# The first group's front of an RWKV-6 block: load order, norm, centering and mixing placed differently

## The chip, the cores and the metric

The kernel runs on one core of one Trainium2 chip. The metric is the device time of one execution in microseconds. Before the change it is 1533.85 us, the median of three runs (1533.52 to 1534.64).

A core has five engines with a queue each, worked in order: TensorE (PE in the profile; its weight loads are shown as PEld), VectorE (DVE), ScalarE (ACT), GpSimd (POOL) and SyncE (SP), which only issues DMAs here. ACT issues some DMAs too. "PEq", "SPq" and the like are the sequencers of the engines.

## The reference

The input is x with 32 sequences of 128 tokens and 512 features, and a context that supplies, for each sequence, two previous rows and a 16 x 512 starting state. All is float32. Cut to what matters:

```python
xn = ln(x) * ln1_w + ln1_b
sx = token_shift(xn, prev)                      # previous row minus this row
xxx = tanh((xn + sx * maa_x) @ maa_w1)          # 5 parts of 32
xxx = matmul(xxx, maa_w2)                       # 5 parts of 512
x5  = xn + sx * (maa_stack + xxx)               # five mixed inputs
w = exp(-exp(time_decay + tanh(x5[1] @ decay_w1) @ decay_w2))
r, k, v = x5[3] @ Wr.T, x5[0] @ Wk.T, x5[2] @ Wv.T
g = silu(x5[4] @ Wg.T)
# per head (32 heads of 16): s is 16 x 16
a = k_t * v_t (outer);  out_t = r_t . (u * a + s);  s = a + w_t * s
att = groupnorm_per_head(out) * gn_w + gn_b
x = x + (att * g) @ Wo.T
xn2 = ln(x) * ln2_w + ln2_b;  sx2 = token_shift(xn2, prev2)
x = x + sigmoid((xn2 + sx2*fmr) @ Wfr.T) * (square(relu((xn2 + sx2*fmk) @ Wfk.T)) @ Wfv.T)
```

## The kernel before, in words

The 32 sequences are worked in eight groups of four. A group's rows are one tile `x` of 128 tokens by 4 x 512 (`load_x`, L283). After the norm everything of the front is held transposed: 128 features on the partitions, four chunks of features (index e or f), and 4 x 128 tokens along the free axis.

For each group there are five generators: `front_mix` (L422) norms, shifts and mixes; `front_proj` (L492) computes the decay w and the projections k, r, v; `front_gate` computes the gate; `prep` (L567) prepares the recurrence; `back` does the group norm, the output projection, the second norm and the feed-forward part. Six more generators do the recurrence over all groups, one unit after another: POOL multiplies k and v (L704) and adds pairs (L708), DVE scans (L726) and multiplies by r (L728), PE sums (L761). Before each instruction a generator yields an `Op`: an engine, a duration in us, the buffers it reads and writes, and sometimes a condition (`need`). `Plan.run` (L138) plays these Ops in a model of the engines when the kernel is built. At each step it takes, among the generators whose next Op could start within EPSILON of the earliest, the one with the smallest due time (`pick`, L177). The due times come from the table DUE (L49): for each kind of generator a begin and an end, in units of groups. So DUE, EPSILON and the durations in the Ops decide the order of the instructions in every queue of the whole kernel; on the chip each engine works that order and waits where data are not there.

The parts that the change touches:

- `load_x` issues one DMA of 1 MB on SP for a group's rows. Two `x` tiles exist.
- `constants` (L247) runs once, in the first group's `front_mix`. It issues the loads of `vec` (all per-feature vectors, L248), `pv` (previous rows, L253), `w1` (L255), the halves of `maa_w2` on SP and on ACT (L259), the decay weights (L262, L264) and `u` (L267), and has POOL compute the four small `ffn` vectors from `vec` (L249 to L252).
- `weight` (L289) issues the load of 1 MB of weights on SP. For the first group `front_proj` asks for wv, wk and wr at once (L497 to L501).
- `center` (L296) subtracts, on POOL, each head's mean from the columns of wv (L303 to L310) and writes the result to DRAM (`dwv`, L312), from where later groups load it.
- `layernorm_T` (L319): for each sequence statistics on DVE (L332, L333); `rstd` on DVE (L350), its power -1/2 on POOL (L352), `nb` on DVE (L354); then the norm, four ACT instructions (L357); a copy of `pv` on ACT (L361); PE transposes chunk by chunk (L377). For each chunk ACT evicts with ln weight and bias into `xnT` (`evict`, L367), then `use` of `front_mix` has ACT do the same in place (L433), DVE subtract to `sx` (L436) and DVE make `xin` (L438, tile `mx`).
- In `front_mix`, PE then multiplies `xin` by `w1` (L444, L397), ACT takes the tanh (L448 to L456), and for each of five inputs m and each pair of chunks PE multiplies by `maa_w2` (L410) and `mixed` (L460) works the two chunks. There are two ways to do one: in groups 1 to 7, for m in `ON_POOL`, DVE does L465 and POOL the addition L467; otherwise DVE does both, L470 and L472. In the first group all five m take the second way.

```python
                if g and m in ON_POOL:
                    nc.vector.scalar_tensor_tensor(x5[:, f, :], p.t, col(V_MAA + m, f), sx[:, f, :], ALU.add, ALU.mult)
                    nc.gpsimd.tensor_tensor(bt(x5[:, f, :]), bt(x5[:, f, :]), row(xnT, f, 1), ALU.add)
                else:
                    nc.vector.scalar_tensor_tensor(p.t, p.t, col(V_MAA + m, f), sx[:, f, :], ALU.add, ALU.mult)
                    nc.vector.tensor_tensor(bt(x5[:, f, :]), bt(p.t), row(xnT, f, 1), ALU.add)
```

Of the kernel before, what the change touches and what calls it, by code (L numbers as in the profile page):

```python
# [19 lines left out]
GB = 4  # L20
# [22 lines left out]
LANDING = 2.0  # L43
HOP = (0.2, 0.05, 0.05, 0.04, 0.08)
ON_POOL = (2, 3, 4)
EPSILON = 0.0388


DUE = {"rec": (0.171, 1.108), "mix": (-4.67, -2.417), "proj": (-4.683, 4.311), "gate": (0.588, 0.608), "prep": (-4.19, 1.684), "back": (-0.012, 3.928), "last1": (-21.388, 9.796), "last2": (10.392, 13.665)}  # L49


class Buf:
# [130 lines left out]
def rwkv6_block(ctx: ExitStack, tc: tile.TileContext, x, prev, s0, vecs, u, maa_w1, maa_w2,  # L183
# [61 lines left out]
    nc.vector.memset(w2p, 0.0)  # L245

    def constants():  # L247
        nc.sync.dma_start(out=vec, in_=vecs)  # L248
        nc.gpsimd.tensor_scalar(ffn[:, 0, :], vec[:, V_FK, :], -1.0, 1.0, ALU.mult, ALU.add)  # L249
        nc.gpsimd.tensor_scalar(ffn[:, 2, :], vec[:, V_FR, :], -1.0, 1.0, ALU.mult, ALU.add)  # L250
        nc.gpsimd.tensor_tensor(ffn[:, 1, :], ffn[:, 0, :], vec[:, V_LN2B, :], ALU.mult)
        nc.gpsimd.tensor_tensor(ffn[:, 0, :], ffn[:, 0, :], vec[:, V_LN2W, :], ALU.mult)  # L252
        nc.sync.dma_start(out=pv, in_=prev)  # L253
        halves = lambda w, h: w.rearrange("r (f h p) -> h r f p", h=2, p=P)[h]
        nc.sync.dma_start(out=w1_sb, in_=maa_w1.rearrange("(c p) o -> p c o", p=P))  # L255
        for m in (1, 0, 2, 3, 4):
            for h, queue in enumerate((nc.sync, nc.scalar)):
                r = h * XD + (XM if m in (1, 3) else 0)
                queue.dma_start(out=w2p[r : r + XM, m, :].rearrange("r (f p) -> r f p", p=P),  # L259
                                in_=halves(maa_w2[m * XM : (m + 1) * XM, :], h))  # L260
            if m == 1:
                nc.sync.dma_start(out=dw1_sb, in_=decay_w1.rearrange("(c p) o -> p c o", p=P))  # L262
                for h, queue in enumerate((nc.sync, nc.scalar)):
                    queue.dma_start(out=dw2p[h * XD : (h + 1) * XD, :].rearrange("r (f p) -> r f p", p=P),  # L264
                                    in_=halves(decay_w2, h))
        for e in range(NE):
            nc.sync.dma_start(out=lanes(u_sb, e), in_=u[e * HE : (e + 1) * HE, :].unsqueeze(0).to_broadcast([GB, HE, S]))  # L267

    def lanes(t, e):


        return t[e::NE]
# [4 lines left out]
    def bt(ap):  # L277
        return ap.rearrange("p (b t) -> p b t", t=L)
# [3 lines left out]

    def load_x(g, need=None, bs=range(GB)):  # L283
        b0, b1 = bs[0], bs[-1] + 1
        (xt,) = yield Op(SP, 0.4, w=[(0, None)], alloc=["x"], xfer=part(4.5, bs), need=need)
        nc.sync.dma_start(out=xt[:, b0:b1, :], in_=x[g * GB + b0 : g * GB + b1].rearrange("b t e -> t b e"))
        return xt
# [27 lines left out]
    def part(us, bs):  # L315

        return us if len(bs) == GB else us * len(bs) / GB + 0.03

    def layernorm_T(g, src, sums, vw, vb, which, use, take, need=None, bs=range(GB)):  # L319
# [33 lines left out]
        (nb,) = yield Op(DVE, 0.16, r=[(mv, None), (rstd, None)], w=[(0, None)], alloc=["nb"], port=True, end=[mv])  # L353
        nc.vector.scalar_tensor_tensor(nb[:, bsl], mean, -1.0 if sums is None else 1.0, rstd[:, bsl], ALU.mult, ALU.mult)  # L354
        for b in bs:
            yield Op(ACT, 0.8, r=[(src, b), (nb, None), (rstd, None)], w=[(xh, b)])
            nc.scalar.activation(xh[:, b, :], src[:, b, :], AF.Identity, bias=nb[:, b : b + 1],  # L357
                                 scale=rstd[:, b : b + 1])
# [4 lines left out]
        late = []  # L363

        def evict(e, pt):
            yield Op(ACT, part(0.78, bs), r=[(pt, None)], w=[(xnT, e)])
            nc.scalar.activation(xnT[:, e * GB + b0 : e * GB + b0 + nb_, 1 : L + 1], bt(pt[:, cols]), AF.Identity,  # L367
                                 bias=col(vb, e), scale=col(vw, e))
            yield from use(xnT, e, pt, tiles)

        for e in range(NE):
# [50 lines left out]
    def front_mix(g, d):  # L422

        xt = yield from load_x(g, (lambda: "x1" in data[g - 3]) if g > 2 else (lambda: "xin" in data[0]) if g else None)
        if g == 0:
            yield Op(SP, 5.5, xfer=4.0)
            yield Op(ACT, 3.9)
            constants()
        need = (lambda: "ln2" in data[g - 3]) if g > 2 else None
        def use(xnT, e, pt, tiles):  # L430

# [7 lines left out]

        xnT, sx, xin = yield from layernorm_T(g, xt, None, V_LN1W, V_LN1B, 0, use, ("sx", "mx"), need)  # L440
        d["xin"] = True
        (pm,) = yield Op(PE, 8 * PASS, r=[(xin, None)], w=[(0, None)], alloc=["ps"])
        for c in range(NE):
            nc.tensor.matmul(pm.t, lhsT=w1_sb[:, c, 0 : 4 * XM], rhs=xin[:, c, :], start=(c == 0), stop=(c == NE - 1))  # L444
# [15 lines left out]
        def mixed(m, i, pp, x5):  # L460

            for f, p in zip((2 * i, 2 * i + 1), pp):
                if g and m in ON_POOL:
                    yield Op(DVE, 0.75, r=[(p, None), (sx, None)], w=[(x5, f)], end=[p])
                    nc.vector.scalar_tensor_tensor(x5[:, f, :], p.t, col(V_MAA + m, f), sx[:, f, :], ALU.add, ALU.mult)  # L465
                    yield Op(POOL, 1.08, r=[(xnT, None)], w=[(x5, f)], port=True)
# [25 lines left out]
    def front_proj(g, d):  # L492
# [507 lines left out]
```

## Time and profile before

| | |
|---|---|
| runs | 1533.85 us (1533.52 to 1534.64) |
| profiled execution | 1535.0 us, of which the span of the instructions is 1533.2 |
| mean granted TensorE clock | 0.959 |
| busy: PE, DVE, POOL, ACT | 1410.0, 1270.9, 1024.8, 656.2 us |
| rows of group 0: issue, first use | 0.72, 6.12 us |
| last `xin` of group 0 done | 26.23 us |
| first mixing instruction on DVE | 37.51 us |
| first projection (k) | 62.52 us |
| first recurrence instruction (POOL L704) | 109.16 us |
| last group's recurrence done, about | 1451 us |

The profile is one execution. Its instructions have a start (us from the start of the span), a duration, the engine, the line of the kernel and the tiles, written before "<-" and read behind it. What ended an engine's idle time is inferred from semaphores. The chain that ended last is followed back from the last instruction. Matmuls are pipelined and their ends are modelled, so busy time of PE is not time at its peak. A float32 matmul of 128x512 appears as two records.

### The profile page before, as it was taken

How to read it: one execution, taken by the hardware profiler on the slowest of the kernel's cores; microseconds unless marked ns; L12 is line 12 of the kernel's file. 1: busy time of each engine (PE TensorE's matmuls, PEld its weight loads, DVE VectorE, ACT ScalarE, POOL GpSimd, SP SyncE). 2: the span in 40 equal slices, each digit the busy share in tenths (PEclk: the TensorE clock that was granted, in tenths of full speed). 3: DMA queues.
4: the chain of work that ended last, by engine and by line, in shares of the span. 5: the costliest groups of instructions: out<-in, count | busy, mean ns of one | idle time of the engine just before them, and what ended most of it. 6: DMA issues, size and time to landing. Idle time of an engine off the chain costs nothing.

```text
span 1533.2 us, 16578 instructions
## 1 busy us (share of the span) xinstructions
PE 1410.0 (92%) x5344; PEld 746.6 (49%) x5344; DVE 1270.9 (83%) x1618; ACT 656.2 (43%) x1277; POOL 1024.8 (67%) x632
## 2 busy tenths in 40 slices
PE   3997898899999999999999999999999998778788
PEld 1343454455554555455554555455544555455444
DVE  5537789989998899899988899899988898878732
ACT  4233242423743356323743365424733354344242
POOL 3014893877787859687786959686777959678400
PEclk9798899899999999999999999999999999889879
DMA  6120331244304431244304521343305421400220
GB/s 223 42 84 23 104 108 29 78 132 145 117 11 144 144 131 43 79 133 142 117 29 134 183 92 35 97 140 124 110 32 163 126 89 41 159 27 28 93 71 28
DMA packets 127559, 146.88 MB, mean 96 GB/s; under 512 B 8176, under 2 KB 77296, under 8 KB 126448
## 3 DMA queue, kind: packets, MB, share of 16 engines
q1 hardware_dynamic: 92112, 128.81, 25.6%
q10 hardware_dynamic: 35360, 17.02, 3.9%
q8 instruction: 42, 0.69, 0.2%
q14 instruction: 45, 0.37, 0.1%
HBM read 94.41 MB, written 17.83 MB: 73 GB/s over the span
## 4 chain that ended last, share of the span: by engine, by line
PE 51%; DVE 27%; POOL 13%; issue 6%; DMA 2%; ACT 1%; SPq 1%; DVEq 0%; POOLq 0%; ACTq 0%
PE ps L391 18%; PE acc L761 8%; POOL am L704 7%; PE ps L939 6%; PE ps L923 6%; PE ps L410 6%; DVE sc L726 5%; POOL a L708 4%; DVE rm L728 4%; PE ps L849 2%; DVE rk L642 2%; DVE ps L634 2%; PE ps L397 2%; PE ps L444 2%; DVE ps L470 1%
## 5 line engine op out<-in xcount | busy, mean ns | idle before, releaser
L704 POOL TENSOR_TENSOR am<-v,k 128x1024 f32<-128x1024 f32 x256 | 610.3, 2384 | 88.7 <-DMA r<-blk 70.4
L391 PE MATMUL ps<-mx,wt 128*128 128x512 f32 (+1 forms) x1312 | 583.2, 593 | 8.8 <-DVE mx L472 3.4
L708 POOL TENSOR_TENSOR a<-am 128x504 f32<-128x504 f32 x256 | 286.1, 1118 | 201.5 <-DVE sc L726 181.1
L391 PEld LDWEIGHTS ps<-mx,wt 128*128 128x128 f32 x1312 | 244.3, 194 | 276.2 <-issue 259.1
L728 DVE TENSOR_TENSOR rm<-sc,r 128x1024 f32<-128x1024 f32 x256 | 312.9, 1222 | 38.3 <-PE acc L761 22.9
L726 DVE TENSOR_TENSOR_SCAN sc<-sc,a 128x512 f32<-128x512 f32 x256 | 313.4, 1224 | 32.7 <-POOL a L708 30.5
L761 PE MATMUL acc<-by_head,rm 128*128 128x128 f32 x2176 | 290.8, 283 | 36.0 <-DVE rm L728 29.9
L761 PEld LDWEIGHTS acc<-by_head,rm 128*128 128x128 f32 x2176 | 252.3, 146 | 135.9 <-issue 54.4
L679 ACT COPY sc<-w 128x512 f32<-128x512 f32 x256 | 151.4, 591 | 219.5 <-DVE rm L728 197.0
L690 ACT COPY a<-st 128x8 f32<-128x8 f32 x256 | 52.2, 204 | 180.1 <-DVE sc L726 156.4
L467 POOL TENSOR_TENSOR mx<-mx,xnT 128x512 f32<-128x512 f32 x84 | 99.7, 1198 | 40.9 <-DVE mx L465 40.3
L923 PE MATMUL ps<-wt,mx 128*128 128x512 f32 x256 | 115.7, 595 | 0.0
L540 ACT COPY blk<-ps 128x512 f32<-128x512 f32 x96 | 56.0, 584 | 137.6 <-PE ps L391 137.6
L849 PE MATMUL ps<-wt,mx 128*128 128x512 f32 x256 | 112.8, 598 | 0.6 <-DVE rk L642 0.6
L410 PE MATMUL ps<-tha,w2p 64*128 64x512 f32 x256 | 89.1, 677 | 18.0 <-DVE mx L472 12.0
L939 PE MATMUL ps<-wt,ev 128*128 128x512 f32 x224 | 102.4, 600 | 2.7 <-DVE mx L472 2.7
L352 POOL TENSOR_TENSOR rstd<-rstd,mhalf 128x4 f32<-128x4 f32 (+1 forms) x17 | 20.2, 1191 | 120.1 <-DVE rstd L350 120.1
L470 DVE SCALAR_TENSOR_TENSOR ps<-ps,vec,sx 128x512 f32<-128x512 f32 x76 | 57.3, 753 | 36.7 <-PE ps L410 36.3
L465 DVE SCALAR_TENSOR_TENSOR mx<-ps,vec,sx 128x512 f32<-128x512 f32 x84 | 61.8, 743 | 21.8 <-PE ps L410 21.7
L849 PEld LDWEIGHTS ps<-wt,mx 128*128 128x128 f32 x256 | 48.9, 192 | 62.5 <-issue 56.5
L923 PEld LDWEIGHTS ps<-wt,mx 128*128 128x128 f32 x256 | 46.4, 190 | 51.0 <-issue 46.8
L939 PEld LDWEIGHTS ps<-wt,ev 128*128 128x128 f32 x224 | 40.9, 192 | 45.3 <-issue 39.9
(108 smaller groups left out, 1341.1 us busy)
## 6 DMA issues: line engine op xcount, KB each, us to landing
x<-in_x SPq DMA_DIRECT2D x15, 1024.0 KB
wt<-in_wk SPq DMA_DIRECT2D x8, 1024.0 KB
wt<-in_wr SPq DMA_DIRECT2D x8, 1024.0 KB
wt<-in_wg SPq DMA_DIRECT2D x8, 1024.0 KB
dgate<-blk SPq DMA_DIRECT2D x32, 256.0 KB
wt<-in_wo SPq DMA_DIRECT2D x8, 1024.0 KB
wt<-in_fk SPq DMA_DIRECT2D x8, 1024.0 KB
wt<-in_fr SPq DMA_DIRECT2D x8, 1024.0 KB
```

What stands on the lines that cost most here:

```text
L391: nc.tensor.matmul(p, lhsT=w[:, c, e * P : (e + 1) * P], rhs=xin[:, c, cols], start=(c == 0), stop=(c == NE - 1))
L410: nc.tensor.matmul(p.t, lhsT=w[h, :], rhs=t[h, :], start=True, stop=True)
L467: nc.gpsimd.tensor_tensor(bt(x5[:, f, :]), bt(x5[:, f, :]), row(xnT, f, 1), ALU.add)
L679: nc.scalar.copy(sc.t, d["w01"][:, q : q + 1, :].to_broadcast([P, DH, T2]))
L704: nc.gpsimd.tensor_tensor(am.t, v[:, ds, :], k[:, q : q + 1, :].to_broadcast([P, DH, L]), ALU.mult)
L708: nc.gpsimd.tensor_tensor(a[:, :, 1:T2], am2[:, :, 0 : T2 - 1, 0], am2[:, :, 0 : T2 - 1, 1], ALU.add)
L726: nc.vector.tensor_tensor_scan(scf, scf, a.t.rearrange("p d n -> p (d n)"), 0.0, ALU.mult, ALU.add)
L728: nc.vector.tensor_tensor(pair(rm.t), sc.t.unsqueeze(3).to_broadcast([P, DH, T2, 2]), r2[:, q : q + 1, :, :].to_broadcast([P, DH, T2, 2]), ...
L761: nc.tensor.matmul(acc[:, i, :], lhsT=rm[:, i, :], rhs=by_head, is_transpose=True, start=(q == 0 and i % 4 == 0), stop=(q == S), skip_grou ...
L849: nc.tensor.matmul(p.t, lhsT=att[:, c, b * L : (b + 1) * L], rhs=wot[:, c, :], start=(c == 0), stop=(c == NE - 1))
L923: nc.tensor.matmul(p.t, lhsT=xr[:, c, b * L : (b + 1) * L], rhs=frt[:, c, :], start=(c == 0), stop=(c == NE - 1))
L939: nc.tensor.matmul(p2.t, lhsT=kv[:, c, b * L : (b + 1) * L], rhs=fvt[:, c, :], start=(c == 0), stop=(c == NE - 1))
```

## The change

Seven edits, all but the last for the first group only:

- Its rows are loaded in two DMAs: sequences 0 and 1 on SP, 2 and 3 on ACT. `vec` and `pv` follow on ACT's queue.
- `constants` no longer issues `vec`, `pv` and `u` and no longer computes `ffn`; wv is asked for only after the constants, and `u` after the weights of the first group (in `prep`).
- The `ffn` vectors are computed by `of_norm2`, behind the norm.
- The norm of sequences 1 and 3 is done by DVE, that of 0 and 2 by ACT.
- The eviction with ln weight and bias is done by DVE in place of ACT.
- In the mixing of every m, the odd chunks take the way with the addition on POOL.
- DUE and EPSILON have other values. (The condition of `center` on "xin" is as it was.)

```diff
-EPSILON = 0.0388
+EPSILON = 0.039
-DUE = {"rec": (0.171, 1.108), "mix": (-4.67, -2.417), "proj": (-4.683, 4.311), "gate": (0.588, 0.608), "prep": (-4.19, 1.684), "back": (-0.012, 3.928), "last1": (-21.388, 9.796), "last2": (10.392, 13.665)}
+DUE = {"rec": (0.171, 0.811), "mix": (-4.351, -2.486), "proj": (-6.56, 7.24), "gate": (0.525, 0.545), "prep": (-4.001, 1.375), "back": (-0.209, 3.178), "last1": (-27.722, 1.84), "last2": (7.448, 22.404)}
...
     def constants():
-        nc.sync.dma_start(out=vec, in_=vecs)
-        nc.gpsimd.tensor_scalar(ffn[:, 0, :], vec[:, V_FK, :], -1.0, 1.0, ALU.mult, ALU.add)
...
-        nc.sync.dma_start(out=pv, in_=prev)
...
-        for e in range(NE):
-            nc.sync.dma_start(out=lanes(u_sb, e), in_=u[e * HE : (e + 1) * HE, :].unsqueeze(0).to_broadcast([GB, HE, S]))
+    def of_norm2():
+        nc.gpsimd.tensor_scalar(ffn[:, 0, :], vec[:, V_FK, :], -1.0, 1.0, ALU.mult, ALU.add)
+        nc.gpsimd.tensor_scalar(ffn[:, 2, :], vec[:, V_FR, :], -1.0, 1.0, ALU.mult, ALU.add)
+        nc.gpsimd.tensor_tensor(ffn[:, 1, :], ffn[:, 0, :], vec[:, V_LN2B, :], ALU.mult)
+        nc.gpsimd.tensor_tensor(ffn[:, 0, :], ffn[:, 0, :], vec[:, V_LN2W, :], ALU.mult)
...
     def load_x(g, need=None, bs=range(GB)):
+        if g == 0:
+            (xt,) = yield Op(SP, 0.4, w=[(0, 0), (0, 1)], alloc=["x"], xfer=2.3)
+            nc.sync.dma_start(out=xt[:, 0:2, :], in_=x[0:2].rearrange("b t e -> t b e"))
+            yield Op(ACT, 1.4, w=[(xt, 2), (xt, 3)], xfer=2.3)
+            nc.scalar.dma_start(out=xt[:, 2:4, :], in_=x[2:4].rearrange("b t e -> t b e"))
+            nc.scalar.dma_start(out=vec, in_=vecs)
+            nc.scalar.dma_start(out=pv, in_=prev)
+            return xt
...
         for b in bs:
+            if g == 0 and sums is None and b % 2:
+                yield Op(DVE, 0.5, r=[(src, b), (nb, None), (rstd, None)], w=[(xh, b)], port=True)
+                nc.vector.tensor_scalar(xh[:, b, :], src[:, b, :], rstd[:, b : b + 1], nb[:, b : b + 1], ALU.mult, ALU.add)
+                continue
...
         def evict(e, pt):
+            if g == 0 and sums is None:
+                yield Op(DVE, 0.69, r=[(pt, None)], w=[(xnT, e)])
+                nc.vector.tensor_scalar(xnT[:, e * GB + b0 : e * GB + b0 + nb_, 1 : L + 1], bt(pt[:, cols]), col(vw, e), col(vb, e), ALU.mult, ALU.add)
+            else:
...
...
         if g == 0:
-            yield Op(SP, 5.5, xfer=4.0)
+            yield Op(SP, 5.0, xfer=4.0)
             yield Op(ACT, 3.9)
             constants()
+            d["constants"] = True
...
         d["xin"] = True
+        if g == 0:
+            yield Op(POOL, 0.9)
+            of_norm2()
...
-                if g and m in ON_POOL:
+                if m in ON_POOL if g else f % 2:
...
         if g == 0:
-            ws[2] = yield from weight(wv)
+            ws[2] = yield from weight(wv, lambda: "constants" in d)
             plan.add(center(ws[2]), -1.0, -0.9, 8)
             ws[0] = yield from weight(wk)
             ws[3] = yield from weight(wr)
+            d["weights"] = True
...
     def prep(g, d):
+        if g == 0:
+            yield Op(SP, 2.5, need=lambda: "weights" in d)
+            for e in range(NE):
+                nc.sync.dma_start(out=lanes(u_sb, e), in_=u[e * HE : (e + 1) * HE, :].unsqueeze(0).to_broadcast([GB, HE, S]))
```

More of the change, by code (lines that the diff above doesn't have):

```diff
@@ L247, in constants @@
     def constants():
-        nc.sync.dma_start(out=vec, in_=vecs)
[L249 to L252, printed above, removed]
-        nc.sync.dma_start(out=pv, in_=prev)
         halves = lambda w, h: w.rearrange("r (f h p) -> h r f p", h=2, p=P)[h]
@@ L365, in evict @@
         def evict(e, pt):
-            yield Op(ACT, part(0.78, bs), r=[(pt, None)], w=[(xnT, e)])
-            nc.scalar.activation(xnT[:, e * GB + b0 : e * GB + b0 + nb_, 1 : L + 1], bt(pt[:, cols]), AF.Identity,
-                                 bias=col(vb, e), scale=col(vw, e))
+            if g == 0 and sums is None:
+                yield Op(DVE, 0.69, r=[(pt, None)], w=[(xnT, e)])
+                nc.vector.tensor_scalar(xnT[:, e * GB + b0 : e * GB + b0 + nb_, 1 : L + 1], bt(pt[:, cols]),
+                                        col(vw, e), col(vb, e), ALU.mult, ALU.add)
+            else:
+                yield Op(ACT, part(0.78, bs), r=[(pt, None)], w=[(xnT, e)])
+                nc.scalar.activation(xnT[:, e * GB + b0 : e * GB + b0 + nb_, 1 : L + 1], bt(pt[:, cols]), AF.Identity,
+                                     bias=col(vb, e), scale=col(vw, e))
             yield from use(xnT, e, pt, tiles)
```

## The prediction

> **What bounds the kernel now.** I read the engine totals first, then the busy time by stretch, then the chain that ended last for the first 130 us, then the instructions in order of time there, and last the waits. The totals and four stretches (columns: stretch, its length, busy time and instruction count of PE, PE's weight loads, DVE, ACT, POOL, the granted TensorE clock, DMA share, GB/s):
>
> ```profile
> PE 1410.0 (92%) x5344; PEld 746.6 (49%) x5344; DVE 1270.9 (83%) x1618; ACT 656.2 (43%) x1277; POOL 1024.8 (67%) x632
> ...
> 37.50:62.50 25.00, 20.39 (x48) 6.67 (x48) 20.84 (x33) 10.16 (x17) 1.01 (x1) 0.70 0.16 43
> ...
> 109.20:300.00 190.80, 164.30 (x605) 82.07 (x603) 157.98 (x189) 66.36 (x140) 133.93 (x81) 0.90 0.21 64
> 300.00:1250.00 950.00, 931.86 (x3651) 493.09 (x3650) 870.38 (x1099) 437.70 (x851) 720.83 (x437) 0.99 0.33 107
> 1250.00:1451.00 201.00, 168.98 (x702) 102.00 (x699) 160.78 (x171) 83.75 (x163) 154.07 (x91) 0.93 0.21 70
> ```
>
> From 300 to 1250 us TensorE is busy 931.9 of 950 us (98.1%): that middle holds only 18 us in which a late start could be caught up. So a start that comes earlier moves the whole middle, and with it the end. The start itself is not bound by TensorE. Instructions in order of time (start, duration, engine, line, tiles; in brackets the engine's idle time and what ended it):
>
> ```profile
> 6.12 0.69 DVE L332 BATCH_NORM_STATS2 stats<-x 128x6 f32<-128x512 f32 x1 [3.94 <-DMA x<-in_x]
> ...
> 9.44 0.17 DVE L350 TENSOR_SCALAR rstd<-mv 128x4 f32<-128x4 f32 x1
> ...
> 11.13 0.19 POOL L249 TENSOR_SCALAR ffn<-vec 128x4 f32<-128x4 f32 x1 [8.88 <-DMA vec<-in_vecs]
> ...
> 11.87 1.02 POOL L352 TENSOR_TENSOR rstd<-rstd,mhalf 128x4 f32<-128x4 f32 x1
> ...
> 12.87 2.32 POOL L303 TENSOR_TENSOR am<-wt 128x1024 f32<-128x1024 f32 x1
> 12.93 2.27 DVE L354 SCALAR_TENSOR_TENSOR nb<-mv,rstd 128x4 f32<-128x4 f32 x1 [3.31 <-POOL rstd L352]
> ...
> 15.24 2.93 ACT L357 ACTIVATE x<-x,nb,rstd 128x512 f32<-128x512 f32 x4 [7.71 <-DVE nb L354]
> ...
> 25.48 0.75 DVE L438 SCALAR_TENSOR_TENSOR mx<-sx,vec,ps 128x512 f32<-128x512 f32 x1
> ...
> 30.18 0.69 DVE L332 BATCH_NORM_STATS2 stats<-x 128x6 f32<-128x512 f32 x1 [3.95 <-DMA x<-in_x]
> ```
>
> Three things are to be seen. The power (L352) is ready to run at 9.61 and runs at 11.87, behind four `ffn` instructions that wait for `vec`. The tiny `nb` instruction takes 2.27 us, where its later executions take 0.15 to 0.16: it ends with POOL's 2.32 us L303, which began 0.06 us before it. And at 26.23 DVE stops for 3.95 us for the rows of the second group, then takes the statistics of groups 1 and 2, before it mixes group 0. The chain shows what that costs (start, length, what):
>
> ```profile
> 21.10 9.05 DMA x<-in_x
> 30.18 0.70 DVE stats L332
> ...
> 37.60 0.67 DVE ps L470
> ...
> 62.52 15.92 PE ps L391 x32
> ```
>
> Mixing starts at 37.51, the first projection (k) at 62.52. In between TensorE has a granted clock of 0.70 and waits for DVE:
>
> ```profile
> PEld ps L410 <- DVE mx L472: 20.4, 11, 7.9
> ```
>
> POOL's recurrence starts at 109.16, when the lanes of v have landed.
>
> **Part by part.** *Rows on two queues.* The one load is issued at 0.72 and its statistics start at 6.12. The Trainium skill ("DMA: Bandwidth & Descriptors", section "Rules for kernel authors") speaks against this edit: spreading loads over issuing engines gives no bandwidth, since all run on the same 16 DMA engines; only issue time is saved. Issue is 0.44 us here. By the trace alone one could hope for half of the transfer, some 1.3 us (1 MB at about 400 GB/s is 2.6 us; 376 GB/s is what the stretch from 20 to 30 us moves). I take the rule: both halves land at about 6.1, gain 0; behind SP's half now stands 0.3 MB of `w1` in place of 1 MB of `wv`, so no loss is seen either. Range 1 us either way.
>
> *Vectors ahead of weights, `ffn` behind the norm.* The power runs at 9.65 instead of 11.87 and ends at 10.67. The centering is placed behind it in POOL's queue, and `wv` is issued behind the constants, so at 10.7 no long POOL instruction runs: `nb` takes 0.16 and ends at 10.86 instead of 15.20. Gain 4.3 (2.2 of wait for `vec`, 2.1 of collision). The 10 us of centering and the 0.8 of `ffn` (4 x 0.2) move behind; their cover is long, since the centered weights are first used at 83.9 and `ffn` after the first recurrence. If `wv` were in by 10.7, L303 would collide again: 2.3 lost. ACT issues three more DMAs (0.44 + 0.34 + 0.34 = 1.1 us). Its own old ones begin only at 2.21, so most of this lies in idle time; it is free at about 6.2 with a table load of 1.28 behind, and first needed at 10.9. If ACT were held up as SP was (4.4 us, 1.72 to 6.11), its half of the norm would be 1 us late.
>
> *`u` moved.* Its four issues (2.42 us on SP, 15.21 to 17.63) go behind wk and wr, before the states and x of groups 1 and 2. First use is L639 at 122.9, so nothing waits; the weights come 2.4 us sooner, the rows behind them do not.
>
> *Norm shared.* Four ACT instructions of 0.73 (2.93 in all) become two on ACT, 1.47, beside two on DVE. No row has this DVE form; the nearest at that size is L472 with 0.69, a floor is half of it; two take 0.7 to 1.4, hidden beside ACT. Gain 1.5.
>
> *Eviction on DVE.* Until now ACT carries two instructions per chunk (0.77 + 0.75) and DVE two (0.69 + 0.75); from the first eviction (18.73) to the last `xin` (26.23) it is 7.5 us. Now DVE carries 0.69 + 0.69 + 0.75 = 2.13, four times 8.5. ACT's part waits for DVE's read, but the next eviction can fill that gap on DVE. Loss 1.0, up to 2.5 if the gaps stay open. Last `xin` at 10.86 + 1.47 + 0.56 (transposes, as from 18.17 to 18.73) + 8.6 = 21.5, so 4.7 us sooner than 26.23.
>
> *Statistics of groups 1 and 2 ahead of the mixing.* From the last `xin` to the first mixing pair TensorE and the tanh need 4.1 us (26.23 to about 30.3), so DVE could mix at 25.6. The eight statistics take 7.3 us (30.18 to 37.43). If they stay ahead and x1 is there by 21.5, mixing starts at 29.0. x1 was issued at 21.10 because SP stood still for 7.7 us (1.72 to 6.11, 6.45 to 8.41, 8.75 to 10.13) behind x and wv before it could issue the constants. Now `vec` and `pv` are on the other queue and a smaller half of x is ahead: I put the constants' issue (5.1 us) at about 2 to 8, the three weights and x1 behind them (4 MB at 376 to 400 GB/s, 10.6 us) at about 10 to 21, with landing 20 to 23. Ends for the start of mixing: 25.6 (the order puts the mixing first) and 33 (both sets of rows late). I take 29.0, near the first, as the data need little more than the time there is: gain 8.5, ends 4.5 and 11.9; the 4.7 from above is in it.
>
> *Additions on POOL.* For odd f the addition (L472) leaves DVE. Rows from the groups that do so already, and from those that don't:
>
> ```profile
> L467 POOL TENSOR_TENSOR mx<-mx,xnT 128x512 f32<-128x512 f32 x84 | 99.7, 1198 | 40.9 <-DVE mx L465 40.3
> ...
> L465 DVE SCALAR_TENSOR_TENSOR mx<-ps,vec,sx 128x512 f32<-128x512 f32 x84 | 61.8, 743 | 21.8 <-PE ps L410 21.7
> ...
> L472 DVE TENSOR_TENSOR mx<-ps,xnT 128x512 f32<-128x512 f32 x76 | 52.6, 691 | 2.6
> ```
>
> The Trainium skill ("GPSIMD Engine Reference", section "Engine selection") says: elementwise work belongs on VectorE, GPSIMD is about twice as slow with two inputs. The rows confirm the ratio (1.20 against 0.69), and by the rule each half that moves would take 0.51 us longer, 10 halves 5 us. But DVE is what TensorE waits for here, and POOL is idle from 38.8 to 109: a pair costs DVE 0.75 + 0.69 + 0.75 = 2.19 instead of 2.88, and POOL's 1.20 lies within it. L465 is no slower beside POOL than L470 without (0.743, 0.753). Eight pairs ahead of the k projection save 5.5 us; the last two, between 78 and 93, where TensorE waits 3 us, some 0.5. I take 6.0, ends 3 (waits for TensorE, 3.6 us in this stretch now, grow) and 7. Queued behind POOL's additions can be the power of a later group; its norm is used at 95 and later.
>
> *Due times.* Eight pairs and EPSILON change, so the order changes everywhere, not in number or kind of instruction. The trace can't show the new order. I take 0; ends: a gain of 10 (TensorE has 26.5 us idle between 109 and 300, at a clock of 0.90) and a loss of 20 (the middle at 96% instead of 98.1%).
>
> **Sum.** 8.5 + 6.0 = 14.5 us at the start of the recurrence (109.2 becomes 94.7), ends 7.5 and 18.9, passed on whole. The profiled execution took 1535.0 (span 1533.2 and 1.8 around it): 1520.5. It lay 1.15 above the median shown (1533.85), so 1519.
>
> **Rivals.** *x1 still late.* The wait moves with the front. For: 9.05 us of DMA stood in the chain, and no byte is saved. Against: SP's 7.7 us of standing still. Gain 4.5 + 3 = 7.5: 1526.
>
> *The order helps too.* Front as above and 10 us of the bubbles between 109 and 300: 1509. For: DVE (158 of 191) and TensorE (164) wait for each other there. Against: nothing in the edit adds an engine there.
>
> *The front is hidden.* Recurrence earlier, end not. For: from 1250 on TensorE idles 32 of 201 us. Against: the recurrence that paces that stretch starts from the same first group. 1532, no change.
>
> *Slower: the new order leaves TensorE idle in the middle.* One mechanism: an instruction placed early on an in-order queue holds those behind it. It decides once the middle's busy share falls by 14.5/950, below 96.6%; at 96% the loss is 20: 1533.85 - 14.5 + 20 = 1539.
>
> **How the numbers follow.** Likeliest 0.58 (own range 1514 to 1525), x1 late 0.13, order helps 0.12, hidden 0.05, slower 0.12. About 0.2% (3 us) is what a measurement of this kernel can tell from no change: faster 0.58 + 0.13 + 0.12 = 0.83, same 0.05, slower 0.12. The range 1507 to 1532 leaves out the slower case and a rest of the third.
>
> **What would show it.** `nb` at about 10.7 with 0.16 us; last `xin` near 21.5; first L470 or L465 of group 0 between 25.6 and 30; about 2.2 us of DVE per mixing pair; k projection near 48; first L704 near 95; the middle at 98%. The prediction is wrong if DVE again waits for x1 beyond 25, if `nb` collides again, or if the middle falls under 97%.

## The result, and the profile after

The changed kernel takes 1522.71 us (median of 4 runs, 1521.47 to 1523.82); the kernel before, run beside it, 1533.81. The ratio is 0.9927, 95% interval 0.9909 to 0.9944: 11.1 us or 0.7% faster. The forecast was 1519, so 14.8 us were expected and 11.1 came. The profiled execution took 1523.82 us, its span is 1522.0.

The totals and the stretches that answer to those of before (stretch, length, busy time and count of PE, weight loads, DVE, ACT, POOL, granted TensorE clock, DMA share, GB/s):

```profile
PE 1407.3 (92%) x5344; PEld 746.5 (49%) x5344; DVE 1264.1 (83%) x1614; ACT 652.7 (43%) x1271; POOL 1036.0 (68%) x642
...
34.30:55.00 20.70, 17.24 (x49) 6.44 (x49) 17.76 (x31) 8.58 (x16) 9.60 (x9) 0.84 0.10 27
55.00:100.20 45.20, 42.78 (x106) 18.56 (x106) 12.08 (x16) 13.77 (x22) 3.98 (x3) 0.92 0.30 85
...
300.00:1250.00 950.00, 931.67 (x3665) 493.54 (x3664) 865.11 (x1095) 440.61 (x856) 715.58 (x434) 1.00 0.33 108
```

The middle is as full as it was (931.67 against 931.86 of 950 us). Most of the gain (8.9 of 11.2 us between the two profiles) is there when the recurrence starts at about 100 us: mixing of the first group takes 20.7 us instead of 25.0 (34.3 to 55.0), and POOL has ten more instructions, the moved additions. The front in order of time (start, duration, engine, line, tiles; in brackets the idle time before and what ended it):

```profile
5.81 0.69 DVE L339 BATCH_NORM_STATS2 stats<-x 128x6 f32<-128x512 f32 x1 [3.63 <-DMA x<-in_x]
...
10.51 0.16 DVE L361 SCALAR_TENSOR_TENSOR nb<-mv,rstd 128x4 f32<-128x4 f32 x1 [1.21 <-POOL rstd L359]
10.71 1.00 DVE L365 TENSOR_SCALAR x<-x,rstd,nb 128x512 f32<-128x512 f32 x2
...
13.18 0.81 DVE L380 TENSOR_SCALAR xnT<-ps,vec 128x512 f32<-128x512 f32 x1 [1.47 <-PE ps L394]
14.81 0.69 DVE L454 TENSOR_TENSOR sx<-xnT,ps 128x512 f32<-128x512 f32 x1 [0.82 <-ACT ps L451]
15.53 0.75 DVE L456 SCALAR_TENSOR_TENSOR mx<-sx,vec,ps 128x512 f32<-128x512 f32 x1
...
24.56 0.75 DVE L456 SCALAR_TENSOR_TENSOR mx<-sx,vec,ps 128x512 f32<-128x512 f32 x1
28.00 0.69 DVE L339 BATCH_NORM_STATS2 stats<-x 128x6 f32<-128x512 f32 x1 [2.69 <-DMA x<-in_x]
...
34.35 0.72 DVE L491 SCALAR_TENSOR_TENSOR ps<-ps,vec,sx 128x512 f32<-128x512 f32 x1
```

`nb` is there at 10.51 and takes 0.16, as forecast. But the last `xin` ends at 25.31, only 0.9 sooner than before, and DVE waits again for the second group's rows (`x1` below): until 28.00, only 2.2 sooner. Seven of the eight statistics then stand ahead of the mixing, which starts at 34.35 in place of 37.51. The chain that ended last shows what is late (start, length, what):

```profile
11.93 9.69 DMA wt<-in_wr
21.64 0.53 SPq L599
...
22.21 5.77 DMA x<-in_x
```

The load of `x1` was issued at 22.21; before it was 21.10. The reordering had made the issue of these rows later, not sooner. SP's queue in order of time shows where it stood:

```profile
11.93 0.51 SPq L298 DMA_DIRECT2D wt<-in_wr  x1
12.48 2.47 SPq L594 DMA_DIRECT2D u_sb<-in_u  x4
14.99 7.17 SPq L599 DMA_DIRECT2D st<-in_s  x4
22.21 1.00 SPq L293 DMA_DIRECT2D x<-in_x  x2
```

All three weights are issued by 12.5. The four small state loads (L599, 32 x 256 each) then take 7.17 us where the four of `u` take 2.47, and `x1` stands behind them. SP's waits name their releasers (in total, times, longest):

```profile
SPq L599 <- DMA wt<-in_wr: 2.2, 1, 2.2
...
SPq L599 <- DMA wt<-in_wk: 2.2, 1, 2.2
...
SPq L599 <- DMA wt<-in_wv: 0.7, 1, 0.7
```

A state load has no data from a weight. The program's list of SP's instructions tells why it waits (position, line, transfer, and in brackets the semaphore that it waits for):

```
10 L298 DMACopy wt_111<-in_wv 128x4x512 [waits DMAHW2_49]
11 L298 DMACopy wt_115<-in_wk 128x4x512 [waits DMAHW3_49]
12 L298 DMACopy wt_117<-in_wr 128x4x512 [waits DMAHW4_49]
...
18 L599 DMACopy st_130<-in_s 32x1x256 [waits DMAHW2_49]
19 L599 DMACopy st_130<-in_s 32x1x256 [waits DMAHW3_49]
20 L599 DMACopy st_130<-in_s 32x1x256 [waits DMAHW4_49]
21 L293 DMACopy x_185<-in_x 128x4x512 [waits DMAHW5_49]
```

In this program the loads issued by SP and ACT take eight completion semaphores in rotation: a load signals the one that it waited for, and it waits until the last load with that semaphore has landed. So wv, wk and wr hold numbers 2, 3 and 4. The eight small loads of `u` and of the states turn this rotation once around, so the second, third and fourth state load wait for wv, wk and wr, and the rows wait behind them. In the kernel before, where `u` went out ahead of wk and wr, the semaphores of the four state loads had last been used by two halves of `maa_w2` and two loads of `u`; they took 2.34 us (18.71 to 21.05). There, too, SP's three early stops were such waits:

```profile
SPq L248 <- DMA x<-in_x: 4.4, 1, 4.4
...
SPq L253 <- DMA w2p<-in_maa_w: 1.9, 1, 1.9
...
SPq L255 <- DMA dw2p<-in_decay_w: 1.4, 1, 1.4
```

`vec` waited for the semaphore of x (1.72 to 6.11), `pv` and `w1` for those of two small loads that ACT had issued. None waited for wv.

To compare all kernels, six columns: start of the first group's mixing, of the k projection and of the first recurrence on POOL, the span, and the time from that recurrence to the end (one profiled execution each), then the ratio of times to the kernel before, with its interval.

| kernel | mixing | k | recurrence | span | rest | ratio |
|---|---|---|---|---|---|---|
| before | 37.51 | 62.52 | 109.16 | 1533.2 | 1424.0 | 1 |
| after | 34.35 | 54.98 | 100.26 | 1522.0 | 1421.7 | 0.9927 [0.9909, 0.9944] |
| a0, after once more | 34.19 | 54.20 | 102.36 | 1523.5 | 1421.1 | 0.9930 [0.9918, 0.9942] |
| a1, eviction back on ACT | 34.30 | 53.79 | 99.64 | 1522.8 | 1423.2 | 0.9927 [0.9914, 0.9939] |
| a2, rows ahead of `u` and states | 31.70 | 53.57 | 98.84 | 1521.8 | 1423.0 | 0.9902 [0.9887, 0.9917] |
| a3, a1 and a2, rows ahead of wk, wr too | 28.73 | 49.33 | 94.99 | 1517.8 | 1422.8 | 0.9898 [0.9882, 0.9914] |
| a4, mixing delayed by 11.5 us | 45.85 | 65.40 | 109.51 | 1536.5 | 1427.0 | 1.0005 [0.9997, 1.0013] |
| a5, additions back on DVE | 33.89 | 57.35 | 102.76 | 1523.8 | 1421.0 | 0.9945 [0.9931, 0.9958] |
| b1, before, additions on POOL | 37.58 | 58.28 | 106.58 | 1527.6 | 1421.0 | 0.9963 [0.9950, 0.9975] |
| b2, before, new due times | 44.86 | 65.89 | 113.57 | 1613.7 | 1500.1 | 1.0514 [1.0500, 1.0529] |
| a6, after, old due times | 35.53 | 54.98 | 103.19 | 1616.6 | 1513.4 | 1.0506 [1.0487, 1.0525] |
| b3, before, the front's edits | 35.44 | 57.28 | 105.56 | 1530.1 | 1424.5 | 0.9958 [0.9946, 0.9971] |
| b4, b3 with a3's two edits | 29.92 | 51.46 | 99.43 | 1520.5 | 1421.1 | 0.9914 [0.9901, 0.9926] |
| a7, a3, second norm later | 27.00 | 47.86 | 93.28 | 1514.0 | 1420.7 | 0.9870 [0.9856, 0.9884] |

Where a ratio is told in us below, it is its distance from 1, or from another ratio, times 1533.85. Where no edit of the order is involved, "rest" runs from 1420.7 to 1427.0 with no order that follows the edits, so differences of 2 or 3 us in it are not put down to anything here.

### The profile page after: what moved, and what is told of

The parts are those of the page before. It is cut to its first block, busy times and chain, and to the rows that moved or that the text cites. A ratio compares the mean times of both kernels' runs of the same rounds, so it can differ in the third digit from the quotient of the medians.

```text
span 1522.0 us, 16610 instructions
## 1 busy us (share of the span) xinstructions
PE 1407.3 (92%) x5344; PEld 746.5 (49%) x5344; DVE 1264.1 (83%) x1614; ACT 652.7 (43%) x1271; POOL 1036.0 (68%) x642
## 3 DMA queue, kind: packets, MB, share of 16 engines
q1 hardware_dynamic: 91312, 127.59, 25.4%
## 4 chain that ended last, share of the span: by engine, by line
PE 51%; DVE 21%; POOL 18%; issue 5%; ACT 3%; DMA 2%; SPq 0%; POOLq 0%; DVEq 0%; ACTq 0%
PE ps L408 18%; POOL am L730 10%; PE acc L787 8%; PE ps L965 6%; POOL a L734 6%; PE ps L949 6%; PE ps L427 5%; DVE sc L752 4%; DVE rm L754 3%; PE ps L875 2%; PE ps L414 2%; PE ps L465 2%; DVE rk L668 1%; DVE ps L660 1%; POOL mx L488 1%
## 5 line engine op out<-in xcount | busy, mean ns | idle before, releaser
L730 POOL TENSOR_TENSOR am<-v,k 128x1024 f32<-128x1024 f32 x256 | 609.0, 2379 | 34.2 <-DMA r<-blk 15.6
L488 POOL TENSOR_TENSOR mx<-mx,xnT 128x512 f32<-128x512 f32 x94 | 111.6, 1198 | 72.9 <-DVE mx L486 68.7
L486 DVE SCALAR_TENSOR_TENSOR mx<-ps,vec,sx 128x512 f32<-128x512 f32 x94 | 69.0, 743 | 25.3 <-PE ps L427 25.1
L427 PE MATMUL ps<-tha,w2p 64*128 64x512 f32 x256 | 82.2, 674 | 3.4 <-DVE mx L493 3.4
L491 DVE SCALAR_TENSOR_TENSOR ps<-ps,vec,sx 128x512 f32<-128x512 f32 x66 | 49.6, 752 | 31.7 <-PE ps L427 31.3
```

The source lines that it names most:

```text
L427: nc.tensor.matmul(p.t, lhsT=w[h, :], rhs=t[h, :], start=True, stop=True)
L730: nc.gpsimd.tensor_tensor(am.t, v[:, ds, :], k[:, q : q + 1, :].to_broadcast([P, DH, L]), ALU.mult)
```

## The experiments

**The change once more (a0).** No edit.

> The kernel after as it is, on the same chip as the others of this call, as their reference: ratio 0.9927, with a spread of under 0.002.

It gave 0.9930 beside 0.9927. Its first recurrence came 2.1 us later than in the first profile (102.36) with the same instructions: the stretch from k to the recurrence took 48.1 us at a granted clock of 0.87, where the first profile has 45.2 at 0.92. One profile's recurrence is thus good to some 2 us.

**Eviction back on ACT (a1).** The order of all instructions stays; four instructions change engine.

```diff
-                nc.vector.tensor_scalar(xnT[...], bt(pt[:, cols]), col(vw, e), col(vb, e), ALU.mult, ALU.add)
+                nc.scalar.activation(xnT[...], bt(pt[:, cols]), AF.Identity, bias=col(vb, e), scale=col(vw, e))
```

> The kernel after, with the first group's eviction done by ACT again; the order of all other instructions in every queue is that of the kernel after. Theory A (the rows of the second group decide when mixing starts: DVE takes statistics of groups 1 and 2 ahead of it, and waits for those rows): last xin near 20.8 instead of 25.3, DVE then waits some 7 us for x in place of 2.7, first mixing still at 34.3, total within 1 us of 1522.7. Theory B (the longer eviction on DVE is on the path): mixing 4.5 us sooner, total near 1518.

DVE in order of time in a1:

```profile
20.29 0.75 DVE L456 SCALAR_TENSOR_TENSOR mx<-sx,vec,ps 128x512 f32<-128x512 f32 x1
27.96 0.69 DVE L339 BATCH_NORM_STATS2 stats<-x 128x6 f32<-128x512 f32 x1 [6.92 <-DMA x<-in_x]
```

The last `xin` ends at 21.04 instead of 25.31, so the eviction on DVE does cost 4.3 us of its stage. The wait for `x1` grows from 2.69 to 6.92 by the same amount, mixing starts at 34.30 and the ratio is 0.9927. In the change as it was made, what sets the start of mixing is `x1` alone.

**Rows ahead of `u` and the states (a2).**

```diff
         nc.sync.dma_start(out=xt..., in_=x[...])          # load_x, groups 1 and 2
+        while g == 2 and later:
+            later.pop(0)()
...
-                nc.sync.dma_start(out=lanes(u_sb, e), ...)
+                later.append(lambda e=e: nc.sync.dma_start(out=lanes(u_sb, e), ...))
...
-            nc.sync.dma_start(out=lanes(st.t, e)..., in_=s0g[e])
+            issue = lambda e=e: nc.sync.dma_start(out=lanes(st.t, e)..., in_=s0g[e])
+            later.append(issue) if g == 0 else issue()
```

> The kernel after, with the eight small DMAs of u and of the first states issued behind the rows of groups 1 and 2 instead of ahead of them; nothing else is moved. Theory A: the rows of group 1 are issued near 12.5 instead of 22.2, land near 25, DVE no longer waits after the last xin (25.3), mixing starts near 32 (2.3 us sooner), total near 1520.3. Theory B, and a third one (the front does not set the end): total unchanged at 1522.7.

SP's queue and DVE in a2:

```profile
12.37 3.73 SPq L293 DMA_DIRECT2D x<-in_x  x2
16.14 3.85 SPq L596 DMA_DIRECT2D u_sb<-in_u  x4
20.04 7.45 SPq L602 DMA_DIRECT2D st<-in_s  x4
```

```profile
25.36 0.69 DVE L341 BATCH_NORM_STATS2 stats<-x 128x6 f32<-128x512 f32 x1
...
31.70 0.73 DVE L493 SCALAR_TENSOR_TENSOR ps<-ps,vec,sx 128x512 f32<-128x512 f32 x1
```

The same three weights are ahead of the rows, so the same bytes; only eight small loads have moved. The issue of `x1` goes from 22.21 to 12.37, and DVE finds the rows there when the last `xin` ends. Mixing starts at 31.70, 2.7 us sooner. The time is 3.8 us shorter by the ratio (0.9902 against 0.9927); the intervals overlap, so the size of this last step is not settled. It was the waiting of the small loads, not the transfer of the weights, that made `x1` late: the start of mixing shows it. The states still wait at the end of the queue (7.45 us), where nothing is behind them in a hurry.

**Rows ahead of wk and wr as well, eviction on ACT (a3).** The edits of a1 and a2, and:

```diff
-            ws[0] = yield from weight(wk)
-            ws[3] = yield from weight(wr)
+            ws[0] = yield from weight(wk, first=True)     # issued from `later`, ahead of u and states
+            ws[3] = yield from weight(wr, first=True)
```

> The kernel after, with both: eviction on ACT, and the rows of groups 1 and 2 issued right behind wv, ahead of wk, wr, u and the states. Theory A: rows land near 19 to 20, last xin near 20.8, statistics end near 27.3, mixing starts near 27.5 (6.8 us sooner than 34.35), start of the recurrence near 93.5 instead of 100.3, total near 1516. If the front does not set the end: total above 1520.

DVE in a3:

```profile
24.08 1.80 DVE L360 TENSOR_SCALAR rstd<-mv 128x4 f32<-128x4 f32 x1
...
28.73 0.73 DVE L494 SCALAR_TENSOR_TENSOR ps<-ps,vec,sx 128x512 f32<-128x512 f32 x1
```

Mixing starts at 28.73, about where I had forecast it for the change (29.0), and the recurrence at 94.99 (forecast 94.7). Span and ratio, 1517.8 and 0.9898, give 15.4 and 15.6 us of gain where 14.8 had been forecast. With the rows there, the eviction's engine decides when the statistics start: the last `xin` ends at 20.84 and they start at 20.76, against 25.44 and 25.36 in a2. By the ratio this is only 0.6 us better than a2, well within the intervals, though the recurrence starts 3.9 us sooner. Mixing came 1.2 us later than expected for a3: `rstd`, 0.17 us otherwise, took 1.80 and ended within 0.03 us of POOL's centering instruction (22.02, for 3.83 us).

**A delay at the start of mixing (a4).** 18 writes of an unused tile on DVE, ahead of the first mixing pair; all of the reference is still computed.

```diff
             for f, p in zip((2 * i, 2 * i + 1), pp):
+                if g == 0 and m == 1 and f == 0:
+                    for _ in range(18):
+                        nc.vector.memset(idle, 0.0)
```

> The kernel after, with 18 memsets of 128x512 on DVE (an unused tile, about 0.5 us each, some 9 us) ahead of the first mixing instruction of the first group. If the start is passed on whole: total longer by the length of the memsets, near 1531.7. If the middle or the tail can take up a late start: under 1527.

DVE in a4, and its middle stretch:

```profile
43.89 0.48 DVE L487 MEMSET idle<- 128x512 f32 x1 [0.17 <-DVE idle L487]
45.85 0.73 DVE L495 SCALAR_TENSOR_TENSOR ps<-ps,vec,sx 128x512 f32<-128x512 f32 x1
```

```profile
300.00:1250.00 950.00, 931.25 (x3648) 491.32 (x3647) 863.85 (x1093) 438.00 (x850) 716.70 (x435) 1.00 0.34 108
```

The mixing starts 11.5 us later than in the change (45.85 against 34.35), and the time rises by 12.0 us (1.0005 against 0.9927). The middle is as full as ever: a late start moves it as a whole. The runs scattered more than elsewhere (1530.4 to 1540.0 over 21), so the 12.0 is good to about 2 us; that most of it is passed on is beyond that. At the recurrence the two profiles lie only 9.3 us apart (109.51 against 100.26), so the passing on is shown in the total and not at each step.

**Additions back on DVE (a5), and alone in the kernel before (b1).**

```diff
-                    nc.gpsimd.tensor_tensor(bt(x5[:, f, :]), bt(x5[:, f, :]), row(xnT, f, 1), ALU.add)
+                    (nc.gpsimd if g else nc.vector).tensor_tensor(bt(x5[:, f, :]), bt(x5[:, f, :]), row(xnT, f, 1), ALU.add)
```

```diff
-                    nc.vector.scalar_tensor_tensor(p.t, p.t, ..., ALU.add, ALU.mult)
+                    to = x5[:, f, :] if g == 0 and f % 2 else p.t
+                    nc.vector.scalar_tensor_tensor(to, p.t, ..., ALU.add, ALU.mult)
...
-                    nc.vector.tensor_tensor(bt(x5[:, f, :]), bt(p.t), row(xnT, f, 1), ALU.add)
+                    (nc.gpsimd if g == 0 and f % 2 else nc.vector).tensor_tensor(bt(x5[:, f, :]), bt(to), row(xnT, f, 1), ALU.add)
```

> The kernel after, with the additions of the odd chunks in the first group's mixing done by DVE again, in the same order. The sum put 6.0 us on them. If DVE is what TensorE waits for there: first mixing unchanged at 34.3, first k projection and start of the recurrence 5 to 6 us later, ratio to the kernel before near 0.9965 instead of 0.9927. If POOL's longer chain or TensorE's waits take the gain back: under 3 us later.

> The kernel before, with only the additions of the odd chunks in the first group's mixing moved to POOL, in the order of before. If they are worth what the sum says: first mixing unchanged at 37.5, k projection near 57.5, start of the recurrence near 103.5, total 5.5 us under before (ratio 0.9964). If the waits for TensorE grow instead: under 3 us.

The mixing stretch of a5 and that of b1, one each:

```profile
33.90:57.30 23.40, 19.59 (x48) 6.86 (x48) 22.56 (x40) 9.82 (x17) 1.37 (x1) 0.77 0.09 23
```

```profile
37.50:58.20 20.70, 15.54 (x48) 6.14 (x48) 16.05 (x26) 10.24 (x17) 9.25 (x8) 0.83 0.14 39
```

In b1 nothing else changes, and the stretch falls from 25.0 to 20.7 us, as in the change; DVE's work in it from 20.84 to 16.05. Its time falls by 5.7 us. At the start of the recurrence it is only 2.6 us ahead of before. Taken away from the change (a5), they cost 2.8 us by the ratio, where the intervals overlap, and 2.4 to 3.2 at the k projection. Why they are worth less there than in b1 I can't tell from these runs: the stretch of a5 is 1.6 us shorter than that of before. Both kernels agree on the sign, and 5.7 and 2.8 lie no further apart than the intervals of these ratios allow.

**Due times alone (b2), and the change with the old ones (a6).**

```diff
-EPSILON = 0.039
+EPSILON = 0.0388
-DUE = {"rec": (0.171, 0.811), "mix": (-4.351, -2.486), "proj": (-6.56, 7.24), ...}
+DUE = {"rec": (0.171, 1.108), "mix": (-4.67, -2.417), "proj": (-4.683, 4.311), ...}
```

This is the edit of a6; that of b2 is the same in the other direction.

> The kernel before, with only DUE and EPSILON of the kernel after. The start of the recurrence came 8.9 us sooner and the end 11.2. If the new order gives the 2.3 between them: 2.3 us under before (ratio 0.9985). If the order is worth nothing by itself: ratio 1.000. If it suits only the new front: slower than before.

> The kernel after, with DUE and EPSILON of the kernel before. If the new order gives the last 2.3 us: ratio 0.9942 instead of 0.9927. If it is worth nothing: 0.9927. If the old order spoils more than that: over 0.996.

The middle of b2 and of a6, one each:

```profile
300.00:1250.00 950.00, 898.17 (x3457) 474.51 (x3456) 835.55 (x1030) 420.36 (x812) 677.80 (x420) 0.97 0.31 100
```

```profile
300.00:1250.00 950.00, 873.44 (x3415) 463.88 (x3413) 826.96 (x1013) 409.62 (x806) 673.87 (x418) 0.98 0.30 96
```

Both are 5% slower than the kernel before: 79 us (b2) and 78 us (a6), or 89 against the change. TensorE is busy 94.5% and 91.9% of the middle instead of 98.1%. The swapped sets hold the same kinds of instruction in the same number; only the order on each queue differs. So of these two kernels each goes with its own set of due times, and as a single edit the set in the change makes the kernel before much slower. The first thing that goes wrong in b2 is on SP: wv, wk and wr are issued ahead of the first group's rows (0.73, 1.23 and 5.93; the rows at 8.63), so the first statistics start at 16.25 instead of 6.12:

```profile
16.25 0.69 DVE L332 BATCH_NORM_STATS2 stats<-x 128x6 f32<-128x512 f32 x1 [14.07 <-DMA x<-in_x]
```

In the change wv may only be asked for after the constants, so its due times can't do this. Yet b2's recurrence starts only 4.4 us later than before; the other 76 us between the spans come behind it. In a6 one wait grew from 143.1 us (4.7 the longest) in the change to:

```profile
ACT sc L705 <- DVE rm L754: 189.9, 90, 18.9
```

ACT, in order, stands up to 18.9 us at one instruction of the recurrence. I didn't follow the chain further, so what leaves TensorE idle in the middle stays open.

**The front's edits without the new order (b3).** The six edits of the front (two queues, vectors first, `ffn` behind the norm, shared norm, eviction on DVE, additions on POOL) put into the kernel before where it issues its instructions; due times and planned costs stay.

```diff
+        if g == 0:
+            nc.sync.dma_start(out=xt[:, 0:2, :], ...)
+            nc.scalar.dma_start(out=xt[:, 2:4, :], ...)
+            nc.scalar.dma_start(out=vec, in_=vecs)
+            nc.scalar.dma_start(out=pv, in_=prev)
...
-            ws[2] = yield from weight(wv)
+            ws[2] = yield from weight(wv, first=1)        # issued behind the constants; wk, wr alike
...
+            if g == 0 and sums is None and b % 2:
+                nc.vector.tensor_scalar(xh[:, b, :], src[:, b, :], ...)
+                continue
```

> All six edits of the first group's front, put into the kernel before without touching its due times or the plan: every queue keeps the order of before, only the instructions named in the change sit on another engine or at another place. If the front alone gives the gain and the start is passed on: first mixing near 35.4, start of the recurrence near 101.5, ratio 0.995. If the new due times were needed for it: ratio near 1.0 or above.

DVE in b3:

```profile
28.11 0.69 DVE L347 BATCH_NORM_STATS2 stats<-x 128x6 f32<-128x512 f32 x1 [2.65 <-DMA x<-in_x]
...
35.44 0.75 DVE L495 SCALAR_TENSOR_TENSOR ps<-ps,vec,sx 128x512 f32<-128x512 f32 x1
```

The rows land as in the change (28.11 against 28.00), so the late `x1` doesn't come from the due times. All eight statistics stand ahead of the mixing, one more than in the change, which is 1.1 us at its start. The gain is 6.4 us, hardly more than b1's 5.7: by these ratios the front's edits without the additions came to about 1 us in the old order (the intervals are 2 us either way). The change itself, with the new due times and with planned costs that know of the edits, is 4.8 us better than b3; 1.1 of it is the start of mixing.

**The same with the rows first (b4).** b3 without the eviction on DVE, and with wk, wr, `u` and the states issued behind the rows of groups 1 and 2.

```diff
-            ws[0] = yield from weight(wk, first=1)
-            ws[3] = yield from weight(wr, first=1)
+            ws[0] = yield from weight(wk, first=2)        # behind the rows
+            ws[3] = yield from weight(wr, first=2)
```

> As the kernel with the front in the old order, but with the eviction left on ACT and the rows of groups 1 and 2 issued right behind wv, ahead of wk, wr, u and the states. First mixing near 29.7, start of the recurrence near 96.5, ratio 0.9915.

0.9914 against 0.9958, 6.7 us, with a mixing start 5.5 us earlier. The late rows cost the old order as they cost the new one. Against a3, which has the same front, the old order is now 2.5 us behind, with overlapping intervals, and its mixing starts 1.2 us later behind an eighth statistic.

**Half of the statistics behind the mixing (a7).** a3, and for group 2 (the third one) the statistics, the norm's factors and the norm are issued behind the second chunk of the first group's k projection.

```diff
+        do = stash.append if g == 2 and sums is None else lambda f: f()
...
-                nc.vector.bn_stats(stats[:, b, :], src[:, b, :])
+                do(lambda b=b: nc.vector.bn_stats(stats[:, b, :], src[:, b, :]))
...
+                    while g == 0 and m == 0 and e == 1 and stash:
+                        stash.pop(0)()
```

> The kernel after with eviction on ACT and the rows first, and with the statistics and the norm of group 2 put behind the first k matmuls, where DVE stood idle for 13.8 us. First mixing near 26.1 instead of 28.7, start of the recurrence near 92, ratio near 0.988. If TensorE and not DVE sets the mixing by then: no better than 0.9898.

DVE in a7:

```profile
24.18 1.59 DVE L361 TENSOR_SCALAR rstd<-mv 128x4 f32<-128x4 f32 x1
...
27.00 0.75 DVE L495 SCALAR_TENSOR_TENSOR ps<-ps,vec,sx 128x512 f32<-128x512 f32 x1
```

Four statistics in place of seven: mixing starts at 27.00, the recurrence at 93.28, and the ratio is 0.9870; of all the other intervals only a3's touches its own. That is 1515.64 us as measured, 19.9 us below the kernel before and 8.7 below the change. Against a3 that is 4.3 us by the ratio, but 1.7 at the start of mixing and at the recurrence; the rest is open. What holds the mixing there is the second group's norm: its power waits on POOL behind a centering instruction that runs until 25.75.

## Why the prediction was right or wrong

The sum was 8.5 (earlier start of mixing) + 6.0 (additions) = 14.5 us from profile to profile. Measured between the two profiles is 1535.0 - 1523.82 = 11.2: 3.2 at the start of mixing, 5.7 between there and the recurrence (4.4 in the mixing and 1.4 behind it), and 2.3 from the recurrence to the end. The 1.4 and the 2.3 are no larger than differences for which these runs give no cause: 2.9 us in the stretch from k to the recurrence between two executions of the change (a0), 6.3 in the column "rest" without b2 and a6. The total fell inside the range, but by the prediction's own sign ("wrong if DVE again waits for x1 beyond 25") its account of the start of mixing was wrong: DVE waited until 28.00.

- *The step that failed: "I put the constants' issue (5.1 us) at about 2 to 8, the three weights and x1 behind them (4 MB at 376 to 400 GB/s, 10.6 us) at about 10 to 21, with landing 20 to 23."* The reason behind it was that SP had stood still "behind x and wv", and would stand still less. This misread the waits of the kernel before: they name x, `w2p` and `dw2p`, not wv, and none of them for data that `vec`, `pv` or `w1` need. The constants did go out by 10.5 and the weights by 12.5. But what holds SP is the rotation of eight completion semaphores, and `u`, moved behind the weights by this change, is four of the eight small loads that turn it around. I had costed that move at nothing: "the weights come 2.4 us sooner, the rows behind them do not". The rows landed at 28.0. a2 shows that the small loads are the cause: behind the rows, they leave `x1` issued at 12.37 with the same weights ahead. In the terms of the rivals, "x1 still late" is what happened up to the start of mixing: 3.2 us, where it gave 4.5 and the forecast 8.5. Its total, 1526, was too high because more than its 3 us, one end of my bound, came from the additions, and 2.3 us came behind the recurrence.
- *Eviction on DVE, 1.0 lost, "the next eviction can fill that gap".* Wrong, and beyond its bound of 2.5: it lost 4.6. From the first eviction to the last `xin` it was 12.1 us (13.18 to 25.31), forecast 8.5, before 7.5. DVE waits 0.82 us in each chunk for ACT's part and ACT up to 2.3 us for DVE's read, since each chunk's four instructions are issued before the next chunk's first; the eviction took 0.81, not 0.69. The forecast `xin` at 21.5 became 25.31. It cost nothing in the end, as a1 shows (last `xin` at 21.04, the same time): it lay under the wait for `x1`. It would have cost as soon as the rows were early, and a2's mixing at 31.70 is set by it: last `xin` 25.4, then seven statistics.
- *Vectors first, 4.3.* Right at its place: `nb` at 10.51 with 0.16 us (10.7 and 0.16 forecast). But the two steps behind it ate it.
- *Rows on two queues, 0.* Right: statistics began at 5.81 instead of 6.12. The rule of the Trainium skill that I took ("DMA: Bandwidth & Descriptors", "Rules for kernel authors") fits with 0.3 us; the 1.3 us that the trace alone could have suggested did not come.
- *Norm shared, 1.5.* Right in the main: DVE's two take 1.00 beside ACT's, within the bound, and the last norm ends 1.73 us behind `nb` instead of 2.97. ACT was "free at about 6.2" only in the forecast. It stopped from 3.00 to 6.15, at a load that waits for the semaphore of its own half of the rows, issued its last load until 9.55, and had its table loaded at 10.86. As `nb` came at 10.67, this cost 0.2 us; that it cost no more was luck.
- *The statistics ahead of the mixing, 7.3.* Seven ran, 6.35 us. That I left them where they were was right for the change, and a7 shows that this was a choice of the kernel: moving four of them is worth 1.7 us at the recurrence and 4.3 by the ratio against a3.
- *Additions on POOL, 6.0.* The mechanism was right, the size a little high: up to the k projection they saved 4.4 us in the change and 4.3 in b1, where the sum had 5.5. By the totals they are worth 5.7 alone (b1) and 2.8 when taken back (a5). The Trainium skill's rule against it ("GPSIMD Engine Reference", "Engine selection") did not decide, as argued: POOL's 1.20 us lay beside DVE's work.
- *Passed on whole.* Shown in the total: 11.5 us of delay at the start of mixing cost 12.0 (a4).
- *Due times, 0, with -10 and +20 as ends.* In the change they and the planned costs are worth 2.5 to 4.8 us (a3 against b4, the change against b3), of which some 1 us is the start of mixing. My ends were too narrow for the edit by itself: 79 us slower. An order that leaves TensorE idle in the middle is thus real, at four times the price that I gave it. It did not occur in the change, whose edits and order go together.

The range held for the right reason in the larger part (the middle is full, the front is passed on, the additions) and by a cancelling in the rest: 5.3 us too much at the start of mixing, 2.3 us too little behind the recurrence. The cause of those 2.3 stays open, and that they fell on the right side was luck.

## What to carry to other kernels

Before moving small loads, count them: where a program's completion semaphores rotate over all loads, as here, a load waits for whatever took its semaphore one round earlier, so a handful of tiny ones between a big one and an urgent one make the urgent one wait for the big one's landing. An engine that becomes faster or slower beside a late transfer changes nothing (a1) until the transfer is early; then it sets the start (a2 against a3). So the late one goes first. An order found by a planner is tied to the kernel that it was found for; an edit of instructions is to be tried both in its old order and with a new one.

## What the runs showed of the hardware

- The granted clock of one and the same program differs between executions in the partly filled stretch after mixing: 0.92 and 45.2 us in one, 0.87 and 48.1 us in the other, 2.9 us apart.
- POOL's addition and DVE's products of two tiles wait for each other. In the changed kernel:

```profile
74.01 1.22 DVE L608 TENSOR_TENSOR k<-k,w 128x1024 f32<-128x1024 f32 x1
...
74.24 2.02 POOL L488 TENSOR_TENSOR mx<-mx,xnT 128x512 f32<-128x512 f32 x1 [18.46 <-DVE mx L486]
75.17 2.16 DVE L650 TENSOR_TENSOR w<-w 128x1008 f32<-128x1008 f32 x1
```

  The addition is 1.18 elsewhere, the second product was 1.19 before, the first is 1.22 in both kernels. The Trainium skill ("SBUF — State Buffer", "Who interferes with whom") has the shared pair of ports as an exclusive lock: DVE blocked until POOL's end at 76.26 and then 1.19 long would end at 77.45; it ended at 77.33. POOL's 2.02 fits it too: blocked by the first product until 75.23 and then 1.18 long, it would end at 76.41; it ended at 76.26.
- The same pairing caught even a tiny instruction with a single tile as input: `rstd` in a7 took 1.59 us (1.80 in a3) instead of 0.17 while POOL's 128x2048 centering ran (21.92, for 3.83 us), and both ended within 0.02 us of each other.
